# A graph network on one core: edge table stored before other loads, a shortened last edge batch, and moments of layer 3 taken one bank later

## The chip, the cores and the metric

The kernel runs on one core of a Trainium2 chip. The metric is device time in microseconds (us) of one execution; the time before is the median of three runs, 1525.76 us (1524.59 to 1526.87). The core has five instruction queues that run side by side and meet at semaphores: PE (matrix multiply), DVE (vector), ACT (scalar functions and copies), POOL (general purpose, here also the issuer of indirect gathers) and SP (here only an issuer of transfers). Transfers run on 16 DMA engines that all queues share.

## The reference: what is computed

The input is a graph of 3125 nodes with 128 features each and 103125 edges, sorted by destination: 50000 random edges, their reverses, and one loop per node. Four graph layers follow one another, each wrapped as `x = layernorm(x + layer(x))`:

```python
x = _layernorm(x + _L0_gnn_ref(x, src, dst, edge_weight, ...))   # weighted sum of x@W over edges, relu
x = _layernorm(x + _L1_gnn_ref(x, edge_index, ...))              # 4-head attention over edges, skip, norm
x = _layernorm(x + _L2_gnn_ref(x, Wq, Wk, Wv, Wo, edge_index))   # dot-product attention over edges
x = _layernorm(x + _L3_gnn_ref(x, edge_index, ...))              # two mean aggregations, sigmoid
```

All four layers use the same edges. Only layer 0 uses the edge weights.

## The kernel before, in words

The kernel does not gather per edge. It builds two dense 3200 x 3200 matrices in device memory (25 blocks of 128 nodes, the last one padded): `f_ctd`, the edge counts in bf16, and `wd`, the summed edge weights in f32. After that each layer is dense matrix products that stream blocks of these matrices back. If a check at the end fails (a flag), a general path is run instead; with these inputs it is not.

**The start (lines 543 to 652).** `src`, `dst` and the weights are loaded as 127 rows of 816 edges (line 583 and on). DVE and ACT form `tab`, which holds for each edge a key (destination times 25 plus source block), the source within its block, and the weight. `tab` is stored to device memory as `td` in two halves, one on SP's queue and one on ACT's (line 634). PE and DVE work out `row_i`, the row of `td` where each group of five destination nodes begins. Then POOL issues five indirect gathers (line 649), each of 128 runs of 256 consecutive edges, one run for each group. Three tiles hold the results, so the fourth and fifth gather wait for the first and second to be read. Before these gathers stand, in SP's order, the load of `x` (line 643) ahead of SP's half of `td`, and in ACT's order the loads of most of the weights (line 541, the helper `load`); POOL's order has `f_both` (line 729) ahead of the gathers.

**Keys (lines 654 to 697).** For each gather, `keys_of` transposes the edges of the 128 groups on PE and turns them into bf16 keys and three-part bf16 weights on ACT and DVE. The tables of the first two gathers are made before the batches start.

**The batches (lines 814 to 901).** The 640 groups are worked off in 40 batches of 16 (`NW`, `BW`, `NBT`). For a batch, `make` has DVE write two one-hot matrices (line 827: `ohd` for the source within its block, `ohc` for destination and source block) and three weighted copies `wod` of `ohd` (line 836); ACT writes a part of the third copy, 16 pieces a batch (line 845). PE then multiplies one-hots against one-hots: in each of four steps of four groups, 8 products for the counts (line 867) and 24 for the weights (line 875). ACT copies both out of PSUM (lines 880 and 886), and SP stores the weights of every batch (two transfers, line 888) and the counts of every two batches (line 891). The one-hots have two buffers, so DVE works at most one batch ahead of PE. Two jobs run beside the first batches: `xw_of` (x times the weight of layer 0; lines 750 to 756), called after the first and second batch in the program, and `products_of_weights` (lines 733 to 744), called after the third. In the order that the scheduler gave the engines, both begin before the first batch's products.

Meanwhile PE already does layer 0: `add0` loads a finished block row of `wd` in halves of 10 blocks (line 793, three buffers) and multiplies it into five PSUM banks (line 797). The last rows of `wd` are there only after the last batch. Groups beyond number 625 hold no node, since 3125 nodes are 625 groups of five: the last batch, groups 624 to 639, has one group with nodes.

**The end of layer 3 (lines 1563 to 1692).** 25 blocks of the output lie in eight PSUM banks (`GT`: five of four blocks, two of two, one of one). PE finishes the banks one after another. For each bank, `sigmoid` has DVE add the layer's own part (line 1581) and ACT take the sigmoid (line 1584); `total` has DVE add `x` (line 1589), `moments` has it take mean and variance (lines 1595 and 1596). `roots` is a chain of 13 small DVE instructions that finds inverse square roots of 8 or 4 variances by Newton steps; the last five blocks use ACT's square root instead, whose table has to be loaded first. `scaled` normalizes on ACT or DVE, and `store` writes 4 to 8 blocks to the output. The order of DVE and ACT here is written out by hand (`manual_schedule`); `mixed` interleaves two lists of instructions. Everywhere else a scheduler orders each engine, and `issue_after` places something behind a given instruction.

Of the kernel before, what the change touches and what calls it, by code (L numbers as in the profile page):

```python
# [15 lines left out]
P = 128  # L16
N = 3125
# [476 lines left out]
KW = WN * NB  # L494
NBT = NW // BW
Z0 = 20
V1 = 100
# [11 lines left out]
def fast_path(  # L509
# [29 lines left out]
    def load(name, ap, shape):  # L539
        t = cst.tile(shape, F32, name=name)  # L540
        nc.scalar.dma_start(t, ap)
        return t
# [32 lines left out]
    with ExitStack() as st:  # L575
# [66 lines left out]
        nc.vector.tensor_copy(ramp, ramp_i)  # L642
    nc.sync.dma_start(x[:, 0:NF, :], x_in[0 : NF * P, :].rearrange("(b p) d -> p b d", p=P))
    nc.gpsimd.memset(x[:, NF, :], 0.0)
    nc.sync.dma_start(x[0:NR, NF, :], x_in[NF * P : N, :])
    egs = []
    for g in range(NG):
        eg = ep.tile([P, EW // 16, 3, 16], F32, name="eg", bufs=3)
        nc.gpsimd.indirect_dma_start(
            out=eg.rearrange("p a t k -> p (a t k)"), out_offset=None, in_=td,  # L650
            in_offset=bass.IndirectOffsetOnAxis(ap=row_i[:, g : g + 1], axis=0),
        )
        egs.append(eg)

    def keys_of(g):
# [43 lines left out]

    l0_wt = load("f_l0_wt", l0_w, [P, P])  # L700
    l0_br = cst.tile([P, P], F32, name="l0_br")
# [10 lines left out]
    for s, a in enumerate((l1_as, l1_ad)):  # L712
        for h in range(H):
            nc.scalar.dma_start(att[h * C : (h + 1) * C, s * H + h : s * H + h + 1], a[h, :].rearrange("(c o) -> c o", o=1))
    wqt = load("f_wq", l2_wq, [P, P])
# [10 lines left out]
    wyv = cst.tile([P, 2 * P], F32, name="wyv")  # L726
    both = cst.tile([P, P], F32, name="f_both")
    def products_of_weights():
        nc.gpsimd.tensor_tensor(both, gb_row, sb_row, OP.add)
        tw = {}  # L730
        for name, w in (("l1", l1_wt), ("q", wqt), ("k", wkt), ("v", wvt)):
            t = zps.tile([P, P], F32, name="trw", tag="acc3")
            nc.tensor.transpose(t, w, ident)
            tw[name] = ep.tile([P, P], F32, name="tw_" + name)
            nc.scalar.copy(tw[name], t)
        t = zps.tile([P, P], F32, name="trw", tag="acc3")
        nc.tensor.matmul(t[:, 0 : 2 * H], tw["l1"], att, start=True, stop=True)
# [74 lines left out]
    wv_ = wd.rearrange("(w i) (c d) -> w (i c) d", i=WN, d=P)  # L812

    def make(b):
# [7 lines left out]
        def twos(k):  # L822
            k = k[:, b % 8, :, :, :].rearrange("p q w t -> p (q w) t")
            return k[:, :, None, :].to_broadcast([P, 2 * BW, P // 2, 2])

        for o, k in ((ohd, kd2), (ohc, kc2)):
            nc.vector.tensor_tensor(  # L827
                o.rearrange("p w (a t) -> p w a t", t=2), twos(k),
                ramp.rearrange("p (a t) -> p a t", t=2)[:, None, :, :].to_broadcast([P, 2 * BW, P // 2, 2]),
                OP.is_equal,  # L830
            )
        wod = []
        for s in range(3):
            f = of_.tile([P, 2 * BW, P], BF16, name="wod")
            n = 2 * BW if s < 2 else BW
            nc.vector.tensor_tensor(  # L836
                f[:, 0:n].rearrange("p w (a t) -> p w a t", t=2), ohd[:, 0:n].rearrange("p w (a t) -> p w a t", t=2),
                twos(w2[s])[:, 0:n], OP.mult,
            )
            wod.append(f)  # L840
# [14 lines left out]
    for b in range(NBT):  # L855
        ohd, ohc, wod, _ = cur
        cur = make(b + 1) if b + 1 < NBT else None
        if b % SB == 0:
            cs = sp.tile([P, NB, SB * BW * WN], BF16, name="cs")
        ws = sp.tile([P, BW, P], F32, name="ws")  # L860
        for k in range(0, BW, 4):
            cp = cps.tile([P, 4, P], F32, name="cp", tag="cw")
# [8 lines left out]
            for j in range(4):  # L871
                for q in range(2):
                    w = q * BW + k + j
                    for s in range(3):
                        nc.tensor.matmul(  # L875
                            wp[:, j, :], ohc[:, w, :], wod[s][:, w, :], start=(j == 0 and q == 0 and s == 0),
# [6 lines left out]
            )  # L883
            if cur:
                cur[3](k)
            nc.scalar.copy(ws[:, k : k + 4, :], wp)  # L886
        for a, e in ((0, 112), (112, KW)):
            nc.sync.dma_start(wv_[b * BW : (b + 1) * BW, a:e, :].rearrange("w k d -> k w d"), ws[a:e, :, :])
        if b % SB == SB - 1:
            i0 = (b - SB + 1) * BW * WN  # L890
            nc.sync.dma_start(ctd[:, :, i0 : i0 + SB * BW * WN].rearrange("c d i -> d c i"), cs)
        if b < 2:
            for blocks in GB[4 * b : 4 * b + 4]:
                xw_of(*blocks)
        if b == 2:
            products_of_weights()
            acc0 = [zps.tile([P, 4, P], F32, name=f"acc{k}", tag=f"acc{k}") for k in range(Z0 // 4)]
# [564 lines left out]
    with ExitStack() as st:  # L1462
# [135 lines left out]
        def some(name, n, d=F32):  # L1598
            return lp.tile([P, 8], d, name=name)[:, 0:n]

# [42 lines left out]
        by = {}  # L1643
        chain = []
        with tc.manual_schedule(engines={mybir.EngineType.DVE, mybir.EngineType.Activation}):
            for g in range(len(GT)):
                for b in range(NB - HB, NB):
                    add2(last[b], b, g)
                sigmoid(g)
                if g == 2:  # L1650
                    chain = roots(0, 8)
                elif g == 3:
                    scaled(0, 4)
                elif g == 4:
                    chain = roots(8, 8)
                    scaled(4, 4)
                    store(0, 8)
                elif g == 5:
                    scaled(8, 4)
                elif g == 6:  # L1660
                    chain = roots(16, 4)
                    scaled(12, 2)
                mixed(chain[:4])
                total(g)
                mixed(moments(g), chain[4:])
                chain = []
            n = 5
            va = some("var3", n)
            sd = some("sd3", n)
# [58 lines left out]
```

## Time and profile before

| what | us |
|---|---|
| median of three runs (lowest, highest) | 1525.76 (1524.59, 1526.87) |
| profiled execution, its own time | 1526.18 |
| its span in the trace | 1524.3 |
| PE busy, weight loads busy | 1394.6, 1221.3 |
| DVE busy, ACT busy, POOL busy | 984.4, 911.2, 127.3 |
| first gather issued | 22.93 |
| first one-hot begun on DVE | 31.82 |
| last count product begun on PE | 467.81 |
| last block rows of layer 0 in the first five banks | 488.26 to 499.65 |
| PE's last matrix product begun | 1503.28 |
| last store issued | 1517.57 |

The span is the time from the first to the last recorded instruction. Busy times are averages over stages with different limits: DVE is nearly always busy in the first third of the span and PE in the rest. A line of a timeline gives start, duration, engine, line of the kernel, operation, output and inputs, shape, how many instructions are merged into the line, and in brackets how long the engine had been idle and what ended that. A line of waits gives engine, tile and line, what was waited for, the total in us, how often and the longest. A line of windows gives a stretch, its length, the busy time and number of instructions of each engine, the granted clock of PE (1.00 is full speed), the mean busy share of the DMA engines and what they moved in GB/s. Releasers are inferred, so a wait for several things names the one that came last by the profile.

### The profile page before, as it was taken

The numbers are of one execution on the slowest core, as the hardware profiler recorded it, in microseconds if no ns is written. First come the engines' busy times: TensorE is split into PE (matmuls) and PEld (weight loads), VectorE is DVE, ScalarE is ACT, GpSimd is POOL, SyncE is SP. The second block draws the span as 40 slices with busy tenths as digits, with TensorE's granted clock in tenths as the row PEclk, the third lists the DMA queues.
The fourth block names the chain that finished last, engine by engine and source line by source line (L and its number), as shares of the span: only waits on it lengthen the run. The fifth ranks groups of instructions, "written<-read, shape, count | busy, mean of one in ns | idle before, by whom it ended". The sixth has DMA issues, their size and how long they took to land. (4 is left out here: it accounts for less than half of the span.)

```text
span 1524.3 us, 35229 instructions
## 1 busy us (share of the span) xinstructions
PE 1394.6 (91%) x14871; PEld 1221.3 (80%) x14871; DVE 984.4 (65%) x1602; ACT 911.2 (60%) x1864; POOL 127.3 (8%) x162
## 2 busy tenths in 40 slices
PE   4899999999997987899989989899999999999994
PEld 3898999898997876889979979677777774458994
DVE  4999999999991389869978878534464351012006
ACT  2988778888883479878778777454465331023003
POOL 2000000000000023113212311300000000000000
PEclk8999999999999999999999999999999999999997
DMA  6387887887878633444434433332222216503551
GB/s 194 83 214 212 217 219 206 236 219 196 227 211 252 204 103 98 143 122 122 130 120 117 131 91 108 119 114 68 68 61 79 79 65 249 203 32 136 200 186 45
DMA packets 210338, 223.92 MB, mean 147 GB/s; under 512 B 72861, under 2 KB 183976, under 8 KB 209914
## 3 DMA queue, kind: packets, MB, share of 16 engines
q1 hardware_dynamic: 206312, 217.26, 48.6%
q10 hardware_dynamic: 3457, 2.35, 0.6%
q8 instruction: 118, 1.93, 0.5%
q0 software_dynamic: 400, 1.97, 0.4%
q14 instruction: 51, 0.41, 0.1%
HBM read 157.19 MB, written 64.36 MB: 145 GB/s over the span
## 5 line engine op out<-in xcount | busy, mean ns | idle before, releaser
L1244 PE MATMUL acc<-vp,cm 128*128 128x198 bf16 x2500 | 344.4, 252 | 7.4 <-DVE cm L1229 4.6
L1228 ACT ACTIVATE fm<-adr,bas 128x896 bf16<-128x896 f32 (+1 forms) x320 | 286.2, 952 | 67.8 <-DVE cm L1229 63.0
L1239 PE MATMUL acc<-vp,ct 128*128 128x204 bf16 x1250 | 314.6, 255 | 8.5 <-DVE vp L1147 4.5
L1244 PEld LDWEIGHTS <-cm 128*128 128x128 bf16 x2500 | 235.6, 98 | 26.0 <-issue 8.7
L875 PE MATMUL wp<-wod,ohc 128*128 128x128 bf16 x3840 | 243.6, 219 | 7.0 <-ACT cs L880 6.6
L875 PEld LDWEIGHTS <-ohc 128*128 128x128 bf16 x3840 | 224.0, 98 | 8.3 <-issue 8.1
L836 DVE TENSOR_TENSOR wod<-ohd,w 128x4096 bf16<-128x4096 bf16 (+1 forms) x120 | 225.1, 1932 | 0.6 <-PE wp L875 0.6
L1229 DVE TENSOR_TENSOR cm<-fm,ct 128x896 bf16<-128x896 bf16 (+1 forms) x320 | 197.9, 649 | 35.7 <-PE acc L1244 14.6
L845 ACT ACTIVATE wod<-ohd,wu 128x128 bf16<-128x128 bf16 x640 | 197.0, 400 | 0.0
L1384 DVE TENSOR_TENSOR e<-e,ct 128x416 f32<-128x416 f32 (+1 forms) x175 | 108.3, 625 | 106.2 <-ACT e L1383 98.0
L1383 ACT ACTIVATE e<-s,f_nm 128x416 f32<-128x416 f32 (+1 forms) x175 | 109.6, 633 | 97.8 <-PE s L1380 88.7
L1388 PEld LDWEIGHTS acc<-self__8127,e 128*128 128x128 f32 x1250 | 148.3, 193 | 20.6 <-issue 18.8
L1388 PE MATMUL acc<-self__8127,e 128*128 128x129 f32 x1250 | 148.6, 276 | 0.5 <-DVE e L1384 0.5
L1380 PE MATMUL s<-yT,f_xT 128*128 128x416 f32 (+1 forms) x350 | 142.8, 543 | 4.6 <-ACT rt L1360 4.0
L797 PE MATMUL acc<-f_xw,cw 128*128 128x128 f32 x1000 | 119.2, 279 | 7.4 <-DMA cw<-wd 7.4
L1239 PEld LDWEIGHTS <-ct 128*128 128x128 bf16 x1250 | 122.4, 98 | 2.6 <-issue 1.5
L886 ACT COPY ws<-wp 128x512 f32<-128x512 f32 x160 | 93.7, 585 | 49.4 <-PE wp L875 47.9
L797 PEld LDWEIGHTS acc<-f_xw,cw 128*128 128x128 f32 x1000 | 115.8, 195 | 7.6 <-DMA cw<-wd 7.6
L867 PE MATMUL cp<-ohc,ohd 128*128 128x125 bf16 x1280 | 96.7, 218 | 22.2 <-ACT ws L886 18.2
L1380 PEld LDWEIGHTS s<-yT,f_xT 128*128 128x128 f32 x350 | 62.1, 191 | 55.5 <-issue 39.2
L827 DVE TENSOR_TENSOR ohd<-kd,ramp 128x4096 bf16<-128x4096 bf16 x40 | 91.6, 2290 | 21.7 <-PE cp L867 21.1
L1563 PEld LDWEIGHTS <-ct 128*128 128x128 bf16 x1875 | 104.9, 98 | 0.0
(298 smaller groups left out, 1497.1 us busy)
## 6 DMA issues: line engine op xcount, KB each, us to landing
ct<-f_ctd SPq DMA_DIRECT2D x48, 800.0 KB
wd<-ws SPq DMA_DIRECT2D x40, 896.0 KB
ct<-f_ctd SPq DMA_DIRECT2D x150, 224.0 KB
cw<-wd SPq DMA_DIRECT2D x50, 640.0 KB
f_ctd<-cs SPq DMA_DIRECT2D x20, 1000.0 KB
ct<-f_ctd SPq DMA_DIRECT2D x25, 416.0 KB
ct<-f_ctd SPq DMA_DIRECT2D x25, 365.2 KB
cw<-wd SPq DMA_DIRECT2D x25, 320.0 KB
```

What stands on the lines that cost most here:

```text
L797: nc.tensor.matmul(accs[j // 4][:, j % 4, :], cw[:, j - h, :], xw[:, i, :], start=False, stop=(i == NB - 1 and (j % 4 == 3 or j == n - 1)) ...
L836: nc.vector.tensor_tensor(f[:, 0:n].rearrange("p w (a t) -> p w a t", t=2), ohd[:, 0:n].rearrange("p w (a t) -> p w a t", t=2), twos(w2[s] ...
L845: nc.scalar.activation(wod[2][:, BW + w, :], ohd[:, BW + w, :], AF.Copy, scale=w3[:, 1, at : at + 1])
L875: nc.tensor.matmul(wp[:, j, :], ohc[:, w, :], wod[s][:, w, :], start=(j == 0 and q == 0 and s == 0), stop=(j == 3 and q == 1 and s == 2), ...
L1228: nc.scalar.activation(f[:, : n * P], at, AF.Relu, bias=bas[:, c, h : h + 1], scale=UP)
L1229: nc.vector.tensor_tensor(m[:, : n * P], f[:, : n * P], ct[:, : n * P], OP.min)
L1239: nc.tensor.matmul(out_(F1, PW), ct[:, k * P : (k + 1) * P], vp[:, c, hp : hp + 2, :, 2 * F1 : V1], start=(c == 0), stop=False, skip_group ...
L1244: nc.tensor.matmul(out_(0, 2 * F1)[:, j], ms[j][:, k * P : (k + 1) * P], vp[:, c, hp + j, :, 0 : 2 * F1], start=False, stop=(c == NB - 1 a ...
L1380: nc.tensor.matmul(s[:, :m], xT[:, c * P : (c + 1) * P], yT[:, i0 * P + a : i0 * P + a + m], start=True, stop=True)
L1383: nc.scalar.activation(e[:, a : a + m], s[:, :m], AF.Exp, bias=nm[:, q : q + 1], scale=scale)
L1384: nc.vector.tensor_tensor(e[:, a : a + m], e[:, a : a + m], ct[:, a : a + m], OP.mult)
L1388: nc.tensor.matmul(acc[k // 3][:, (k % 3) * (P + 1) : (k % 3 + 1) * (P + 1)], es[q, c][:, k * P : (k + 1) * P], vo[:, c, 0 : P + 1], start ...
```

## The change

There are three parts.

1. **Start.** The load of `x` and, behind it, nearly all weights move to SP's queue and behind the first two gathers; two small writes to `x` on POOL, placed behind the second gather, make the load of `x` wait for it. The weight and bias of layer 0 stay on ACT's queue. `xw_of` is placed behind the last product of batch 0 and of batch 1, and `products_of_weights` behind that of batch 2.
2. **Last batch.** It makes and multiplies 4 groups instead of 16 (`LW`): one step of PE instead of four, and narrower one-hots. The rows of `wd` that it no longer stores are filled with zeros by six transfers at the start, and the columns of `cs` that it no longer writes by one instruction on POOL. The store of the counts keeps its size.
3. **End of layer 3.** The moments of a bank come after the next bank's `sigmoid` part on DVE, ahead of its `total`. The chains of roots are two of eight blocks instead of two of eight and one of four, taken one bank later; the last nine blocks (five before) use ACT's square root. Which blocks are scaled on ACT and DVE, and where the stores stand, changes with that.

```diff
+LW = 4
+NL = (NBT - 1) * BW + LW
...
     def load(name, ap, shape):
         t = cst.tile(shape, F32, name=name)
-        nc.scalar.dma_start(t, ap)
+        with tc.issue_after(x_load.ins):
+            nc.sync.dma_start(t, ap)
         return t
...
-    nc.sync.dma_start(x[:, 0:NF, :], x_in[0 : NF * P, :].rearrange("(b p) d -> p b d", p=P))
-    nc.gpsimd.memset(x[:, NF, :], 0.0)
-    nc.sync.dma_start(x[0:NR, NF, :], x_in[NF * P : N, :])
     egs = []
     for g in range(NG):
         eg = ep.tile([P, EW // 16, 3, 16], F32, name="eg", bufs=3)
-        nc.gpsimd.indirect_dma_start(
+        got = nc.gpsimd.indirect_dma_start(
...
         egs.append(eg)
+        if g == 1:
+
+            with tc.issue_after(got.ins):
+                nc.gpsimd.memset(x[:, 0:1, 0:1], 0.0)
+                nc.gpsimd.memset(x[:, NF, :], 0.0)
+    x_load = nc.sync.dma_start(x[:, 0:NF, :], x_in[0 : NF * P, :].rearrange("(b p) d -> p b d", p=P))
+    nc.sync.dma_start(x[0:NR, NF, :], x_in[NF * P : N, :])
...
-    l0_wt = load("f_l0_wt", l0_w, [P, P])
+    l0_wt = cst.tile([P, P], F32, name="f_l0_wt")
+    nc.scalar.dma_start(l0_wt, l0_w)
...
-            nc.scalar.dma_start(att[h * C : (h + 1) * C, s * H + h : s * H + h + 1], a[h, :].rearrange("(c o) -> c o", o=1))
+            with tc.issue_after(x_load.ins):
+                nc.sync.dma_start(att[h * C : (h + 1) * C, s * H + h : s * H + h + 1], a[h, :].rearrange("(c o) -> c o", o=1))
...
+    none = ep.tile([P, 10 * NB], F32, name="none")
+    nc.vector.memset(none, 0.0)
+    for i in range(NL * WN, NP, 10):
+        with tc.issue_after(x_load.ins):
+            nc.sync.dma_start(wd[i : i + 10, :].rearrange("i k -> (i k)").rearrange("(p k) -> p k", p=P), none)
...
+        def some(s):
+            if b < NBT - 1:
+                return [slice(0, 2 * BW if s < 2 else BW)]
+            return [slice(0, LW)] + ([slice(BW, BW + LW)] if s < 2 else [])
...
+        nw = BW if b < NBT - 1 else LW
         if b % SB == 0:
             cs = sp.tile([P, NB, SB * BW * WN], BF16, name="cs")
+            if b + SB == NBT:
+                nc.gpsimd.memset(cs[:, :, ((SB - 1) * BW + LW) * WN :], 0.0)
         ws = sp.tile([P, BW, P], F32, name="ws")
-        for k in range(0, BW, 4):
+        for k in range(0, nw, 4):
...
-            if cur:
+            if cur and (b + 1 < NBT - 1 or k < LW):
                 cur[3](k)
...
-            nc.sync.dma_start(wv_[b * BW : (b + 1) * BW, a:e, :].rearrange("w k d -> k w d"), ws[a:e, :, :])
+            nc.sync.dma_start(wv_[b * BW : b * BW + nw, a:e, :].rearrange("w k d -> k w d"), ws[a:e, 0:nw, :])
...
         if b < 2:
-            for blocks in GB[4 * b : 4 * b + 4]:
-                xw_of(*blocks)
+            with tc.issue_after(made.ins):
+                for blocks in GB[4 * b : 4 * b + 4]:
+                    xw_of(*blocks)
         if b == 2:
-            products_of_weights()
+            with tc.issue_after(made.ins):
+                products_of_weights()
...
                 sigmoid(g)
-                if g == 2:
-                    chain = roots(0, 8)
-                elif g == 3:
+                if g in (3, 5):
+                    chain = roots(0 if g == 3 else 8, 8)
+                if g == 4:
                     scaled(0, 4)
-                elif g == 4:
-                    chain = roots(8, 8)
+                elif g == 5:
                     scaled(4, 4)
                     store(0, 8)
-                elif g == 5:
+                elif g == 6:
                     scaled(8, 4)
-                elif g == 6:
-                    chain = roots(16, 4)
-                    scaled(12, 2)
-                mixed(chain[:4])
+
+                mixed(left, chain)
+                chain = []
                 total(g)
-                mixed(moments(g), chain[4:])
-                chain = []
-            n = 5
+                left = moments(g)
+            n = 9
             va = some("var3", n)
             sd = some("sd3", n)
+            ms = some("ms3", n)
 
             nc.scalar.activation(some("root3", 1), deg[:, 0:1], AF.Sqrt)
-            scaled(14, 2)
+            scaled(12, 2)
+            mixed(left)
+            nc.vector.tensor_scalar(va, mv[:, 16:25, 1], EPS, None, OP.add)
+            nc.scalar.activation(sd, va, AF.Sqrt)
+            scaled(14, 2, True)
             store(8, 8)
-            nc.vector.tensor_scalar(va, mv[:, 20:25, 1], EPS, None, OP.add)
-            nc.scalar.activation(sd, va, AF.Sqrt)
-            scaled(16, 4, True)
+            nc.vector.reciprocal(sd, sd)
+            nc.vector.scalar_tensor_tensor(ms, mv[:, 16:25, 0], -1.0, sd, OP.mult, OP.mult)
+            for j in range(n):
+                by[16 + j] = sd[:, j : j + 1], ms[:, j : j + 1]
+            scaled(16, 4)
+            scaled(20, 5, True)
             store(16, 4)
-            nc.vector.reciprocal(sd, sd)
-            ms = some("ms3", n)
-            nc.vector.scalar_tensor_tensor(ms, mv[:, 20:25, 0], -1.0, sd, OP.mult, OP.mult)
-            for j in range(n):
-                by[20 + j] = sd[:, j : j + 1], ms[:, j : j + 1]
-            scaled(20, 3)
-            scaled(23, 2, True)
             store(20, 5)
```

More of the change, by code (lines that the diff above doesn't have):

```diff
@@ L824, in twos, with packed @@
             return k[:, :, None, :].to_broadcast([P, 2 * BW, P // 2, 2])
-        for o, k in ((ohd, kd2), (ohc, kc2)):
[L827 to L831, printed above, removed]
+        def some(s):
+            if b < NBT - 1:
+                return [slice(0, 2 * BW if s < 2 else BW)]
+            return [slice(0, LW)] + ([slice(BW, BW + LW)] if s < 2 else [])
+        def packed(o, ww):
+            return o[:, ww].rearrange("p w (a t) -> p w a t", t=2)
+        for o, k in ((ohd, kd2), (ohc, kc2)):
+            for ww in some(0):
+                nc.vector.tensor_tensor(
+                    packed(o, ww), twos(k)[:, ww],
+                    ramp.rearrange("p (a t) -> p a t", t=2)[:, None, :, :].to_broadcast(
+                        [P, ww.stop - ww.start, P // 2, 2]
+                    ),
+                    OP.is_equal,
+                )
         wod = []
@@ L834, in make @@
             f = of_.tile([P, 2 * BW, P], BF16, name="wod")
[L835 to L839, printed above, removed]
+            for ww in some(s):
+                nc.vector.tensor_tensor(packed(f, ww), packed(ohd, ww), twos(w2[s])[:, ww], OP.mult)
             wod.append(f)
@@ L874, in fast_path @@
                     for s in range(3):
-                        nc.tensor.matmul(
+                        made = nc.tensor.matmul(
                             wp[:, j, :], ohc[:, w, :], wod[s][:, w, :], start=(j == 0 and q == 0 and s == 0),
@@ L1598, in some @@
         def some(name, n, d=F32):
-            return lp.tile([P, 8], d, name=name)[:, 0:n]
+            return lp.tile([P, 9], d, name=name)[:, 0:n]
         def roots(b0, n):
@@ L1644, in fast_path @@
         chain = []
+        left = []
         with tc.manual_schedule(engines={mybir.EngineType.DVE, mybir.EngineType.Activation}):
```

## The prediction

> **What bounds the kernel now.** The page's chain of work that ended last is no help here: it holds two pieces, both at 1517 us, and breaks off. I read the stages instead, first by windows, then by timeline, at the three places that the change touches.
>
> The start. In the windows of one microsecond the DMA engines are full from 11 to 20 us; they carry the table `td` (1.25 MB), but also `x` (1.57 MB), which stands ahead of one half of `td` on SP's queue, and weights. The row at 10 us is 0.85 full at only 78 GB/s: there the bias rows are copied to all partitions in pieces of 512 bytes.
>
> ```profile
> 10.00:11.00 1.00, 0.00 (x0) 0.00 (x0) 1.00 (x7) 0.87 (x1) 0.50 (x1) 1.00 0.85 78
> ...
> 13.00:14.00 1.00, 0.83 (x4) 0.84 (x5) 0.00 (x0) 0.11 (x1) 0.00 (x0) 1.00 1.02 313
> ...
> 19.00:20.00 1.00, 0.00 (x0) 0.00 (x0) 0.00 (x0) 0.00 (x0) 0.00 (x0) 1.00 0.96 365
> 20.00:21.00 1.00, 0.47 (x2) 0.47 (x3) 0.00 (x0) 0.00 (x0) 0.00 (x0) 1.00 0.50 186
> ```
>
> The timeline shows who waits. `row_i` is ready at 17.06, yet the first gather goes out at 22.93: it waits for `td` (the profile names another transfer, but in the program the gather waits only for `td` and `row_i`). DVE waits for the second gather until 29.95, and the one-hots begin at 31.82.
>
> ```profile
> 16.89 0.17 DVE L641 TENSOR_SCALAR row_i<-cnt 128x5 int32<-128x5 f32 x1
> ...
> 22.93 1.20 POOL L649 DMA_INDIRECT eg<-td,row_i  x1 [11.20 <-DMA f_att<-in_L_gnn_att_dst_dram]
> ...
> 29.95 0.35 DVE L662 TENSOR_SCALAR kic<-eg,thr 128x256 f32<-128x256 f32 x1 [2.23 <-DMA eg<-td,row_i]
> ...
> 31.82 2.28 DVE L827 TENSOR_TENSOR ohd<-kd,ramp 128x4096 bf16<-128x4096 bf16 x1
> ```
>
> From there to 150 us DVE (third column) is the bound, with ACT behind it; later DVE loses some 7% to waits for PE:
>
> ```profile
> 50.00:100.00 50.00, 45.78 (x696) 44.35 (x694) 49.47 (x32) 44.35 (x126) 0.00 (x0) 1.00 0.65 164
> 100.00:150.00 50.00, 45.10 (x696) 44.05 (x694) 49.83 (x31) 44.90 (x129) 0.00 (x0) 1.00 0.79 211
> 150.00:200.00 50.00, 47.28 (x719) 46.77 (x718) 45.52 (x26) 39.80 (x110) 0.00 (x0) 1.00 0.80 213
> ```
>
> So a start that is earlier by some microseconds moves everything behind it, if ACT keeps up.
>
> The last batch. Its four steps on PE end near 470; SP can store its weights only at 474.5, since it stands until then before a buffer for `cw`; behind that store (1000 KB) and the counts (1000 KB) comes the load that PE waits for, 7.42 us without work. After it PE runs slower: 11.39 us for 80 instructions that took 9.20 before.
>
> ```profile
> 467.81 0.60 PE L867 MATMUL cp<-ohc,ohd 128*128 128x125 bf16 x8
> ...
> 471.64 9.20 PE L797 MATMUL acc<-f_xw,cw 128*128 128x128 f32 x80
> 474.50 3.24 SPq L888 DMA_DIRECT2D wd<-ws  x2
> 477.79 1.37 SPq L891 DMA_DIRECT2D f_ctd<-cs  x1
> 479.26 22.64 SPq L793 DMA_DIRECT2D cw<-wd  x9
> ...
> 488.26 11.39 PE L797 MATMUL acc<-f_xw,cw 128*128 128x128 f32 x80 [7.42 <-DMA cw<-wd]
> ```
>
> The end. PE begins its last products at 1503.28, DVE still has 13 us to go and waits 0.7 us for ACT's sigmoid in most banks:
>
> ```profile
> 1487.89 0.63 ACT L1584 ACTIVATE t<-t 128x512 f32<-128x512 f32 x1 [87.31 <-DVE t L1581]
> 1488.55 0.69 DVE L1589 TENSOR_TENSOR f_xw<-t,f_x 128x512 f32<-128x512 f32 x1 [0.69 <-ACT t L1584]
> ...
> 1517.57 0.87 SPq L1634 DMA_DIRECT2D out_dram<-f_x  x1
> ```
>
> **Part 1, the start: 4.0 us earlier.** With `x` and the weights gone, `td` is alone. Its first half is issued at 12.32; 1.25 MB at the 380 GB/s of the rows from 17 to 20 us are 3.3 us; bytes begin to flow about 1 us behind an issue, and the gather came 2.3 us behind the last full row: 18.9. The edges themselves also land sooner, which can move `td` and `row_i` up by about 1.7 (DVE waited 4.61 for `src`, between weight loads): 17.2 for `td`, and 15.4 for `row_i`, below which it can't go. I take 17: 6 us. Ends 4.0 and 7.5. The second gather should keep its 5.5 us to landing: `x` now starts beside it, the weights are gone.
>
> What that newly leans on: `x` waits on SP for the second gather's issue, and behind `x` stand 24 weight transfers and six zero fills of 128 KB, ahead of batch 0's store. Their bytes fall into 35 to 50 us, where the DMA share was 0.00 to 0.02. ACT's order now has the copies of the third and fourth gather ahead of the rest of the second key table and of the first counts copy. At 300 GB/s `x` and three gathers of 0.4 MB are 9 us from about 19, so 28 to 29, when DVE needs them at 28: at most 1 us, inside the ends.
>
> The price: `xw_of` and the weight products were partly done before 46 us, while ACT had gaps. Now all 14 copies at 0.47 from start to start and seven at 0.3, 8.7 us, lie in batches 1 to 3; before, 4.2 us of them did, with DVE never stalled. Four or five of the copies also wait for their products on PE (four took 0.71 at 41.57). So about 7.5 us more. A batch takes DVE 9.9 us (43.42 to 53.36) and ACT 8.6 (16 pieces in 4.8, eight copies at 0.47), leaving 1.3 a batch or 4 over three batches; the second one-hot buffer gives 2 to 4 more (PE's last step of batch 1 ends at 61.0; DVE needs its buffers at 63.3 and 65.5). 7.5 - 4 - 2 is 1.5; I take 2. Ends 0 and 6. No earlier row shows the new order, hence the wide ends.
>
> **Part 2, the last batch: 7.0 us earlier.** Three steps of PE go, 462.09 to 467.81, 5.7 us; DVE's one-hots (10.2 us a batch) and 12 pieces on ACT shrink too, but DVE was done at 461.7, so PE's count is the one that matters. PE then starts the block row of 471.6 at 466, frees the buffer, and SP gets on at about 469. But the DMA engines are full to 473 (0.92 to 1.12 in the windows) and still have 0.66 MB of `cw` to bring, to about 475. Then 0.25 + 1.0 + 0.64 MB at the 294 GB/s of 476 to 488 are 6.6 us, and about 1 to land: 482.5 in place of 488.26, 5.8 us. Without any backlog it would be 480; if only the smaller store counted (0.75 MB, 2.6) and the idle stretch of 473 to 476 (0.38 busy, 1.9), 4.5. PE's wait shrinks from 7.4 to about 4.5 us. In the trace the granted clock averaged 0.68 over 485 to 488, so it fell at about 486, 5.2 us into the wait; a shorter one may keep it, and then 80 instructions take 9.2 in place of 11.4. I count half: 1.2. Ends of the part: 4.5 and 9.
>
> The Trainium skill, "TensorE: Matmul & The Clock Gate", Part 1, speaks against that half: the array drops to half rate after an idle window of about 3.4 us, and windows run free. A 4.5 us wait would then often still end cold, which makes the part 5.8 and not 7.0. At the end of the kernel the trace agrees with the shorter time (PE stops at 1504.3, 0.66 over 1506 to 1508), in the wait at 481 it took longer.
>
> The zero column fill on POOL costs nothing (POOL idles from 32 to 470, 437.67 us); `none` is written while DVE waits 4.61 us for `src`. If those covers went, it would be under 2 us.
>
> **Part 3, the end: 1.4 us earlier.** Walking DVE with the rows' times (sums 1.0 for four blocks, total 0.65, moments 1.07, a chain of 13 with moments 2.9): banks 1 to 3 start when PE frees them (1490.1, 1493.5, 1496.9); bank 3 with its chain ends at 1501.4, bank 4 at 1504.15, bank 5 with a chain at 1507.9, bank 6 at 1509.4. Bank 7's sigmoid now stands behind four `scaled` on ACT: total at 1511.0 (before 1513.8). Then the table load (1.28), two `scaled`, the root at 1513.1, reciprocal and product to 1513.7, four `scaled` on ACT to 1515.4 beside five on DVE. The last compute ends at 1515.4 in place of 1517.5, but two stores follow (0.87 and 1.1 us of SP), so the last issue ends 0.9 earlier; of the 17 blocks that were stored behind 1515.7 at 290 GB/s, eight now go 2.5 us sooner. I take 1.4; ends 0 and 2.5.
>
> **Sum.** 6.0 - 2.0 + 7.0 + 1.4 = 12.4. The profiled execution took 1526.18 (span 1524.3 and 1.88 around it), so 1513.8; the median stands 0.42 lower: 1513.4. The order of the engines between 500 and 1480 us is as before, so the gain should pass through.
>
> **Rivals.**
> - *All works out* (0.20): ACT's backlog is absorbed, PE stays warm: 7 + 8.5 + 2 = 17.5, 1508.3. For it: no stall of DVE from 43 to 75 us. Against: twice the copies there.
> - *The start is given back* (0.15): ACT's backlog stalls DVE for all 6 us: 7 + 1.4, 1517.4. For it: ACT is at 89% there already.
> - *SP's list comes too late* (0.05, slower): the 30 transfers behind `x` hold batch 0's store. With two `ws` buffers, ACT stalls once that store is not over by about 59, so the list must end by 53, 34 us after `x`: about 1.05 us each. On ACT's queue the weights took 0.44 to 0.5 each, the first four `att` transfers 6.08, 1.52 each. If all took 1.52, the list would take 52 us, 18 too long: 12.4 gained, 18 lost, 1531. It decides at about 1.4 each.
> - *Next to nothing* (0.05): the start is given back and the wait for `cw` stays, so only scraps remain: within 0.2%.
>
> **The numbers.** My forecast has 0.55. The range 1506.5 to 1519.5 takes in the first two rivals and most of the ends, about 8 in 10. Faster by more than 0.2% (3 us, about what a measurement of this kernel can tell from no change): 0.90; within: 0.05; slower: 0.05.
>
> **What would show it.** The first gather at 16 to 18.5; the first one-hot at about 26; DVE's wait for PE or ACT between 45 and 80 us (new, under 3 us in sum, if I am right); PE's wait for `cw` at the end of layer 0 shorter than 5.5 us, with its clock telling whether it stayed warm; one-hot products ending near 460; the last store issued near 1516.5 less the shift. I'm wrong if the first gather still waits beyond 20, if `ws` is late for SP's list, or if the batches after 150 us run slower than 11 us each.

## The result, and the profile after

The changed kernel takes 1524.79 us (median of 14 runs, 1523.01 to 1528.32) and the kernel before 1526.11 us (14 runs beside them). The ratio is 0.9993 with a 95% interval of 0.9986 to 1.0001: no difference that can be told. The forecast was 1513.4, in a range from 1506.5 to 1519.5.

The profiled execution after has a span of 1521.5 us (1524.3 before), 2.8 us shorter. It took 1523.26 us, 1.5 less than its median, so about half of these 2.8 us is the scatter of single executions. Where they come from:

| place | before | after | later (+) or earlier (-) |
|---|---|---|---|
| first gather issued | 22.93 | 19.51 | -3.42 |
| DVE's first one-hot, batch 0 | 31.82 | 28.03 | -3.79 |
| DVE's first one-hot, batch 7 | 104.65 | 109.94 | +5.29 |
| DVE's first one-hot, batch 39 | 451.72 | 456.27 | +4.55 |
| last rows of layer 0 end in the first five banks | 499.65 | 498.19 | -1.46 |
| PE's last bank begun | 1503.28 | 1501.01 | -2.27 |
| last compute instruction ends | 1517.55 | 1512.79 | -4.76 |
| end of the span | 1524.3 | 1521.5 | -2.8 |

So the start gains 3.8 us, loses 9.1 by batch 7, and the last batch gives some 6 back. The lines below answer to those shown of before. First the windows of the kernel after (stretch, length, PE, PEld, DVE, ACT, POOL, clock, DMA share, GB/s):

```profile
11.00:12.00 1.00, 0.67 (x2) 0.50 (x2) 0.80 (x4) 0.04 (x1) 0.00 (x0) 1.00 0.73 157
...
13.00:14.00 1.00, 1.00 (x7) 1.00 (x6) 0.00 (x0) 0.00 (x0) 0.00 (x0) 1.00 1.35 274
...
15.00:16.00 1.00, 0.68 (x3) 0.69 (x4) 0.86 (x5) 0.00 (x0) 0.00 (x0) 1.00 0.02 10
...
17.00:18.00 1.00, 1.00 (x7) 1.00 (x6) 0.00 (x0) 0.00 (x0) 0.00 (x0) 1.00 0.71 294
...
50.00:100.00 50.00, 46.93 (x630) 44.20 (x630) 42.19 (x29) 42.51 (x120) 0.00 (x0) 1.00 0.58 151
```

`td` is alone on the DMA engines now, yet its 1.25 MB take from 11 to 18 us, with a hole at 15. The two halves, 64 packets of 9.8 KB each, moved one behind the other. The rows by queue show it (queue, kind, packets, MB, share of the 16 engines' time; q1 carries what SP issues, q10 what ACT issues). First the kernel after from 11 to 14.5 us and from 14.5 to 18.2:

```profile
q1 hardware_dynamic: 64, 0.63, 86.4%
...
q10 hardware_dynamic: 82, 0.63, 86.9%
```

Before, both queues moved at once, here from 18 to 20 us, at 379 GB/s together. 75 of these 151 packets are larger than 8 KB, as those of `td` are (9.8 KB), and they make up 0.73 of the 0.76 MB:

```profile
q1 hardware_dynamic: 57, 0.43, 59.1%
q10 hardware_dynamic: 94, 0.32, 40.7%
```

SP's half was issued at 10.41 instead of 12.32. ACT's half stands behind other work of ACT, and its issue ended at 13.84 in both kernels; first before, then after:

```profile
13.34 0.50 ACTq L634 DMA_DIRECT2D td<-tab  x1
```

```profile
12.37 1.47 ACTq L637 DMA_DIRECT2D td<-tab  x1
```

DVE, busy for 49.47 of the 50 us from 50 to 100 before, has only 42.19, and ACT, with 42.51, isn't full either. The waits of DVE from 45 to 100 us (what waited, for what, total, times, longest) name the reason, first before, then after:

```profile
DVE ohd L827 <- ACT wod L845: 0.5, 1, 0.5
```

```profile
DVE ohd L851 <- PE cp L893: 7.8, 4, 3.0
```

The timeline of the kernel after at the places that were shown of before:

```profile
19.51 1.20 POOL L649 DMA_INDIRECT eg<-td,row_i  x1 [17.06 <-DMA td<-tab]
...
22.18 0.82 SPq L659 DMA_DIRECT2D f_x<-in_x_dram  x1
...
28.03 2.29 DVE L851 TENSOR_TENSOR ohd<-kd,ramp 128x4096 bf16<-128x4096 bf16 x1
...
30.62 0.40 ACT L677 COPY wei<-eg 128x256 f32<-128x256 f32 x1 [2.25 <-DMA eg<-td,row_i]
...
63.97 2.29 DVE L851 TENSOR_TENSOR ohd<-kd,ramp 128x4096 bf16<-128x4096 bf16 x1 [1.89 <-PE cp L893]
...
79.28 0.27 ACT L751 COPY tw_q<-trw 128x128 f32<-128x128 f32 x1 [0.42 <-PE trw L749]
...
471.68 4.73 PE L813 MATMUL acc<-f_xw,cw 128*128 128x128 f32 x40 [1.17 <-DMA cw<-wd]
479.00 4.73 PE L813 MATMUL acc<-f_xw,cw 128*128 128x128 f32 x40 [2.59 <-DMA cw<-wd]
487.36 10.83 PE L813 MATMUL acc<-f_xw,cw 128*128 128x128 f32 x80 [3.62 <-DMA cw<-wd]
...
1513.34 0.40 SPq L1661 DMA_DIRECT2D out_dram<-f_x  x1
```

ACT's copy of the third gather stands ahead of the second key table and waits 2.25 us, since `x` now moves beside that gather. Each weight product is one step of PE and one copy of ACT in turn (ACT waits 0.42 to 0.58 us ahead of most of these copies of 0.17 to 0.27 us). DVE waits for one-hot buffers that PE frees late. At the end of layer 0 PE waits three times (7.4 us in sum, as before), but starts its last rows 0.9 us sooner than before although DVE reached batch 39 4.55 us later.

### The profile page after: what moved, and what is told of

It reads as the page before. It is cut to its first block, busy times and chain, and to the rows that moved or that the text cites. A ratio compares the mean times of both kernels' runs of the same rounds, so it can differ in the third digit from the quotient of the medians.

```text
span 1521.5 us, 35026 instructions
## 1 busy us (share of the span) xinstructions
PE 1387.3 (91%) x14762; PEld 1214.9 (80%) x14775; DVE 975.9 (64%) x1595; ACT 903.8 (59%) x1845; POOL 129.3 (8%) x164
## 5 line engine op out<-in xcount | busy, mean ns | idle before, releaser
L862 DVE TENSOR_TENSOR wod<-ohd,w 128x4096 bf16<-128x4096 bf16 (+2 forms) x122 | 221.3, 1867 | 0.6 <-PE wp L901 0.6
L851 DVE TENSOR_TENSOR ohd<-kd,ramp 128x4096 bf16<-128x4096 bf16 (+1 forms) x41 | 90.0, 2196 | 28.2 <-PE cp L893 27.9
```

The costliest lines, as they stand in the source:

```text
L862: nc.vector.tensor_tensor(packed(f, ww), packed(ohd, ww), twos(w2[s])[:, ww], OP.mult)
```

## The experiments

Theory A: part 1 gains 3.8 us and pays more than that, because the copies of `xw_of` and of the weight products were moved out of ACT's idle time into the first batches; parts 2 and 3 gain. Rival B: part 1 comes out even and part 2 gains nothing, its wait being bound by transfers. Ratios are to the kernel before on the same chip, and "us to before" is the ratio's share of the median of before. A column named "batch 39" is the start of DVE's first one-hot of that batch in the trace.

**Each part alone.** The first three runs take the change apart, the fourth is parts 2 and 3 together. Where part 1 is out, the zero fills are issued behind the first store of batch 0.

```diff
# e1: part 1 of the diff above alone
# e2: part 2 alone, e4: parts 2 and 3, both with the fills placed so:
-        with tc.issue_after(x_load.ins):
+    if b == 0:
+        with tc.issue_after(put.ins):   # put: the second store of ws
             nc.sync.dma_start(wd[i : i + 10, :]..., none)
# e3: part 3 alone
```

> The kernel before with part 1 alone (edges first, `x` behind the second gather, weights behind `x`, `xw_of` and the weight products behind the last one-hot products of their batches). Theory A (the start gains 3.8 us and the moved copies stall DVE for more than that): DVE's first one-hot 3.8 us sooner, its one-hot of batch 39 about 4.5 us later than before, and the kernel +4.5 us, ratio 1.003. Rival B (part 1 comes out even, and it is part 2 that gains nothing): 0 us, ratio 1.000. The prediction on record (6.0 gained, 2.0 paid): -4 us, ratio 0.9974.

> The kernel before with part 2 alone (the last batch holds four groups; the zero fills of the table are issued behind the first store of batch 0). Theory A: the step is worth 5.5 us of earlier landing of `cw` and 0.5 us of faster products behind it, so -6 us, ratio 0.9961. Rival B (the wait for `cw` is bound by the transfers, since its sum over three waits is 7.4 us as before): 0 to -1 us. The prediction on record: -7 us, ratio 0.9954.

> The kernel before with part 3 alone (moments a bank behind in layer 3's end). Theory A (the last compute ends 2.5 us sooner against PE's last bank, but the stores behind it end only 0.5 us sooner): -0.5 us, ratio 0.9997, not to be told from 1. The prediction on record: -1.4 us, ratio 0.9991. Rival: the new order of the end costs more than it brings, 0 to +1 us.

> Parts 2 and 3 without part 1 (zero fills behind the first store of batch 0). Theory A: -6.5 us, ratio 0.9957, some 5 us faster than the whole change. Rival B (part 2 gains nothing): -0.5 to -1.5 us, like the whole change, ratio 0.9993.

| run | ratio (95%) | us to before | batch 39 |
|---|---|---|---|
| part 1 | 1.0053 (1.0039 to 1.0067) | +8.1 | 456.55 |
| part 2 | 0.9982 (0.9972 to 0.9992) | -2.7 | 453.68 |
| part 3 | 0.9983 (0.9974 to 0.9992) | -2.6 | 451.42 |
| parts 2 and 3 | 0.9965 (0.9952 to 0.9977) | -5.3 | 453.20 |

Part 1 alone makes the kernel slower, so both rival B and the prediction fall; it costs more than theory A said (+4.8 us at batch 39 in its trace as expected, +2.4 more at the end, see below). Part 2 gains half of what was expected, part 3 five times. The trace of parts 2 and 3 tells one reason why part 2 falls short: up to batch 8 it runs with part 3 alone (114.41 and 114.28), and by batch 10 it is 2.6 us behind (137.03 and 134.38). There the scheduler gave PE another order: 40 products of layer 0 in one piece. The PE timeline of parts 2 and 3, and behind it that of part 3 alone:

```profile
120.21 4.68 PE L803 MATMUL acc<-f_xw,cw 128*128 128x128 f32 x40
```

```profile
106.81 2.45 PE L797 MATMUL acc<-f_xw,cw 128*128 128x128 f32 x20
119.11 2.45 PE L797 MATMUL acc<-f_xw,cw 128*128 128x128 f32 x20
```

DVE waits 2.6 us for PE between 105 and 140 us in the first and not at all in the second. Part 2 alone has the long piece too, and 24.2 us from batch 8 to batch 10 where before has 20.1. The changed kernel has a third order, without this loss. That is one reason why the three parts, measured alone, add to +2.8 us and not to the -1.1 of the whole.

**Where part 1 loses.** Four runs move one thing each in the changed kernel.

```diff
# e5: both freed; e6: xw_of alone; e7: the weight products alone
-            with tc.issue_after(made.ins):
-                for blocks in GB[4 * b : 4 * b + 4]:
-                    xw_of(*blocks)
+            for blocks in GB[4 * b : 4 * b + 4]:
+                xw_of(*blocks)
-            with tc.issue_after(made.ins):
-                products_of_weights()
+            products_of_weights()
# e8: x behind the third gather
-        if g == 1:
+        if g == 2:
```

> The kernel after without the ordering of `xw_of` and the weight products behind the batches' products; `x` and the weights still come late. Theory A (the placement behind batches 0 to 2 stalls DVE for 7.4 us, while ACT is without work for 7.7 us between 25 and 45 us): DVE's one-hot of batch 39 5 to 7 us earlier than after (456.27), the kernel 1524.8 - 6 = 1519, ratio 0.995 to before. Rival C (it is the load order that costs: copies in the gaps then wait for `x` and weights that land at 30 to 46 us and stall the key tables): DVE no earlier than after, ratio 0.999 or above.

> The kernel after with `xw_of` alone freed, the weight products still behind batch 2. Theory A: the losses at batches 3 and 4 (2.9 and 1.4 us) go, the 3.0 us at batch 5 stay: DVE at batch 39 4.3 us earlier than after, about 1520.5, ratio 0.9965. Rival C: no earlier than after, 0.999 or above.

> The kernel after with the weight products alone freed, `xw_of` still behind batches 0 and 1. Theory A: the 3.0 us at batch 5 go, the 4.3 us at batches 3 and 4 stay or grow to 5: DVE at batch 39 2 to 3 us earlier than after, about 1522.3, ratio 0.9975. Rival C: 0.999 or above.

> The kernel after with `x` behind the third gather in place of the second. Theory A: the third gather lands 2 us sooner (ACT's copy of it ended DVE's wait at batch 0's second one-hot, 2.0 us); the later `x` costs nothing as `xw_of` stands behind batch 0 in any case: DVE 1 to 2 us earlier at batch 39, ratio 0.998 to 0.999. Rival C (late `x` is what stalls ACT and PE): 1 to 2 us later than after, ratio 1.000.

| run | ratio (95%) | us to before | batch 0 | batch 1 | batch 3 | batch 7 | DVE waits, 45 to 100 us |
|---|---|---|---|---|---|---|---|
| before | 1 | 0 | 31.82 | 43.42 | 63.30 | 104.65 | 0.5 |
| after | 0.9993 (0.9986 to 1.0001) | -1.1 | 28.03 | 41.16 | 63.97 | 109.94 | 7.8 |
| both freed | 0.9973 (0.9964 to 0.9983) | -4.1 | 28.25 | 41.11 | 61.34 | 106.34 | 4.3 |
| `xw_of` freed | 0.9983 (0.9974 to 0.9992) | -2.6 | 28.33 | 41.28 | 61.17 | 106.04 | 3.9 |
| products freed | 0.9998 (0.9989 to 1.0007) | -0.3 | 27.73 | 40.54 | 63.77 | 108.57 | 7.1 |
| `x` behind the third gather | 0.9981 (0.9971 to 0.9990) | -2.9 | 27.85 | 39.73 | 63.58 | 109.56 | 8.9 |

Freeing `xw_of` brings 3.9 us by batch 7, near the 4.3 expected. But 2.4 of them are lost again between batches 7 and 10 (32.72 us for 30.28), where DVE waits 1.9 us for ACT and 0.8 for PE, so that batch 39 comes only 1.4 us earlier. Freeing the products alone brings 1.4 us by batch 7 and nothing at batch 39, 457.05 (expected 2 to 3). With both free DVE still waits 4.3 us, and even then stands 1.7 us behind the kernel before at batch 7: half of theory A holds, and so does half of rival C, as I read it because the copies cannot start before `x` is there. (The profiled execution with both freed took 1528.11 us beside a median of 1523.11, so its later rows are not read.) With `x` behind the third gather the 1.5 us between batches 0 and 1 are won, and most of them lost again at batch 3, where DVE waits longer. So a sooner start only meets the same backlog sooner. The ratio of this run lies where it was expected (0.998 to 0.999), but its interval overlaps with that of the kernel after, and its trace has batch 39 only 0.6 us earlier (expected 1 to 2).

**Can `x` come early and the start too?** And what does the order of parts 2 and 3 cost?

```diff
# e9: parts 2 and 3; zero fills placed behind the first one-hots
+                hot = nc.vector.tensor_tensor(...)            # make, ohd and ohc
+        if b == 0:
+            with tc.issue_after(hot.ins):
+                ...zero fills...
# e10: the kernel after, both freed, x directly behind SP's half of td
+        with tc.issue_after(first_half.ins):
+            x_load = nc.sync.dma_start(x[:, 0:NF, :], ...)
# e11: as e10, and in load():
-        with tc.issue_after(x_load.ins):
-            nc.sync.dma_start(t, ap)
+        with tc.issue_after(stored.ins):
+            nc.scalar.dma_start(t, ap)
```

> Parts 2 and 3 without part 1 as before, but the six zero fills of the table stand behind the first one-hot and not behind batch 0's store. Theory A: parts 2 and 3 alone lost 2.9 us in batches 8 to 10 because the fills behind batch 0's store changed the order that the planner gives PE there (20 products of layer 0 in one place in place of 10 and 10); with the fills earlier that order is as before, so DVE stands at batch 39 as before (451.5 within 0.5) and the kernel gains 5.6 + 2.0 = 7.6 us, ratio 0.995. Rival E (the loss belongs to the shorter last batch or is chance): as in parts 2 and 3 before, DVE at batch 39 near 453.5, ratio 0.9965.

> The kernel after with `x` directly behind its queue's half of `td` (no wait for the second gather) and `xw_of` and the weight products free; weights, zero fills and parts 2 and 3 as after. Theory A (it is the late `x`, that moves 14 copies out of ACT's gaps, that gives the start back): `x` lands near 21 us, first gather near 19.5, first one-hot near 28.5, DVE's waits for PE between 45 and 100 us under 1 us, DVE at batch 39 at 448 to 449.5 (3 us before the kernel before), and the kernel 3 + 5.6 + 2 - 1.7 (the longer end that the runs with part 1 show) = 9 us faster than before, ratio 0.994. Rival D (ACT's work of 44 of 50 us is what stalls DVE once the start is earlier, wherever the copies stand): DVE waits 3 to 5 us there again, batch 39 at 452 to 454, ratio 0.997.

> The same as the run before it, but 16 weight transfers are issued by ACT behind its half of `td` and not by SP. SP then has 515 instructions in place of 530 (the kernel before has 514). Theory A for the end: the time from the last issue of a store to the end of the span, 7.5 to 7.9 us in all runs with part 1 and 5.7 to 6.4 in all without, goes with SP's longer program (a last fetch of instructions stands alone at the end), so it is 5.7 to 6.4 here, and the kernel 1.5 us faster than the run before it, ratio 0.993. Rival F (the end's length has another cause): 7.5 to 7.9. The 16 issues take ACT 7 us between 13 and 24, where it has no other work: no loss, or up to 1 us.

In the second and third of these the last block of `x` is set to zero behind its load, so the features of the last 53 nodes are left out and the result is not that of the reference.

| run | ratio (95%) | us to before | first gather | batch 0 | batch 7 | batch 39 |
|---|---|---|---|---|---|---|
| fills behind the one-hots | 0.9966 (0.9953 to 0.9979) | -5.2 | 23.44 | 34.23 | 106.44 | 453.52 |
| `x` behind `td` | 0.9956 (0.9942 to 0.9969) | -6.7 | 23.52 | 31.77 | 105.14 | 452.19 |
| weights on ACT | 0.9975 (0.9967 to 0.9984) | -3.8 | 22.04 | 34.29 | 107.60 | 455.55 |

The first run has PE's order of before, and the 2.6 us between batches 8 and 10 are gone (116.39 to 136.48, 20.1 us as before). But the fills did not wait for the one-hots: `issue_after` orders SP's list, and with no data to wait for SP issued them at once, beside the first two gathers, so that batch 0 began 2.1 us later than with part 3 alone. Its timeline:

```profile
19.83 4.57 SPq L851 DMA_DIRECT2D wd<-none  x6
23.44 1.20 POOL L651 DMA_INDIRECT eg<-td,row_i  x1 [12.13 <-DMA td<-tab]
...
34.23 2.29 DVE L841 TENSOR_TENSOR ohd<-kd,ramp 128x4096 bf16<-128x4096 bf16 x1
```

So the run ends where its rival E had put it (batch 39 near 453.5, ratio 0.9965), for another reason.

The second run missed its start (first gather expected near 19.5). Its timeline:

```profile
10.10 0.54 SPq L637 DMA_DIRECT2D td<-tab  x1
11.08 0.83 SPq L641 DMA_DIRECT2D f_x<-in_x_dram  x1
...
23.52 1.20 POOL L655 DMA_INDIRECT eg<-td,row_i  x1 [21.06 <-DMA td<-tab]
```

On SP's own queue `x` kept its turn: SP's half of `td` moved from 11 to 14 us, and `x` from there. But the other half, issued by ACT at 12.06, moved only from 18.4 to 22, behind and beside the rest of `x`. These are the rows of ACT's queue from 14 to 18.4 us and from 18.4 to 22:

```profile
q10 hardware_dynamic: 2, 0.00, 0.1%
...
q10 hardware_dynamic: 79, 0.63, 42.5%
```

The first gather, which needs both halves, is back at 23.5, and DVE's waits are back at 0.6 us. In these runs, either `x` moves ahead of ACT's half of `td` and the gather is late, or `x` comes behind the gathers and the copies are late. No run put `x` directly behind both halves, and none had both early, so rival D (a stall even with early copies, once the start is earlier) was not decided by this one.

The third run was expected 1.5 us faster than the second and is slower. The 16 issues kept ACT until 31.87 (expected 24), and its copies for the first key table stand behind them, so batch 0 began at 34.29 although the first gather went out at 22.04.

**The copies left out, and the best version.**

```diff
# e12: the kernel after; in products_of_weights and xw_of, six places like
-            nc.scalar.copy(tw[name], t)
+            nc.gpsimd.memset(tw[name], 0.0)
# e13: parts 2 and 3; the zeros are written behind the last gather
+    with tc.issue_after(got.ins):
+        nc.gpsimd.memset(none, 0.0)
# (the six fills follow, with no order of their own)
```

> The kernel after without the copies of `xw_of` and of the weight products: GpSimd fills their results with zeros at the start instead, so that layer 0's output, layer 1's attention and layer 2's products are computed from zeros; the products on TensorE stand where they stood. Theory A (those 21 copies on ACT, and PE's waiting for them, are the whole 7.4 us that DVE loses in batches 3 to 5): DVE's waits for PE between 45 and 100 us fall from 7.8 to under 1 us, its one-hot of batch 39 comes 6 to 7.5 us earlier than after (449 to 450), the kernel 6 to 7 us faster than after, ratio 0.995. Rival G (the load order and the third gather cost it, not the copies): DVE waits 4 us or more there still, batch 39 at 453 or later.

> Parts 2 and 3 without part 1, the zero fills waiting for the issue of the last gather (GpSimd writes their zeros behind it). Theory A: no fill beside the first two gathers (which cost the run with early fills 2.1 us at the first one-hot) and PE's order in batches 8 to 10 as before: first one-hot near 32, batch 39 at 451.5, the kernel 5.6 + 2.0 = 7.6 us faster than before, 1519, ratio 0.995. Rival E (the loss moves elsewhere again): 0.9965 as in the two runs before it with parts 2 and 3.

| run | ratio (95%) | us to before | batch 0 | batch 7 | batch 39 |
|---|---|---|---|---|---|
| copies left out | 0.9941 (0.9924 to 0.9957) | -9.0 | 28.04 | 103.26 | 449.76 |
| fills behind the gathers | 0.9957 (0.9945 to 0.9969) | -6.6 | 32.16 | 104.38 | 451.45 |

Without the copies batch 39 comes 6.5 us earlier than after, as theory A expected. DVE's waits fall from 7.8 to 2.6 us, not to under 1; the remaining 2.6 us I put down to the products themselves, which still lie between those of the batches, but that was not tried. Rival G falls: of the 9.1 us lost between batches 0 and 7, the copies account for 6.7. The DVE waits of this run, 45 to 100 us:

```profile
DVE ohd L851 <- PE cp L893: 2.6, 2, 1.6
```

The last run does as expected up to batch 39 (batch 0, batch 39 and the fills at 32.89), and has the lowest ratio of those that compute the reference: 1520.76 us, against 1526.76 for the kernel before beside it. It leaves the start as it was and takes parts 2 and 3. From batch 39 to the end of layer 0's last rows it gains 4.1 us, not the 5.6 expected. Its lead over the earlier run with parts 2 and 3 is not shown: it is 1.75 us ahead at batch 39, but its span is 1.0 us longer (1520.4 for 1519.4), and the two intervals overlap.

**The end.** From the end of the last store's issue to the end of the span it took 5.7 to 6.5 us in the seven kernels in which SP issues 506 to 520 transfers (before, parts 2, 3, 2 and 3, and e9, e11, e13), and 7.5 to 8.1 us in the eight in which it issues 530 to 536 (after, part 1, e5 to e8, e10, e12). The transfers of the last microseconds differ. First the kernel after, from 1515.5 us on in 40 slices, then parts 2 and 3 from 1513.5 (GB/s in each slice):

```profile
GB/s 47 129 22 69 22 22 22 22 3 0 0 0 0 0 0 0 50 0 0 0 0 0 0 0 0 0 0 0 0 50 0 0 0 0 0 0 0 0 0 0
q14 instruction: 5, 0.04, 2.1%
```

```profile
GB/s 265 277 284 299 296 299 211 50 44 28 69 72 69 22 22 22 22 3 0 0 0 0 0 0 0 0 50 0 0 0 0 0 0 0 0 0 0 0 0 0
q14 instruction: 4, 0.03, 1.8%
```

When the output has landed, two single fetches of instructions follow in the kernel after, some 2.1 us apart, and only one without part 1. Moving 16 issues from SP to ACT took the time from 8.1 (e10) to 6.5 us (e11), which speaks for the length of SP's program as the cause, with theory A for the end; that the second fetch is one of SP's is not shown. From PE's last bank to the end it is 21.02 us before, 18.87 to 19.11 in the four runs with part 3 and without part 1, 23.38 with part 1 alone and 20.49 in the whole change. So part 3 gains some 2.0 us by itself, and the whole change keeps 0.5 of them.

## Why the prediction was wrong

**The reading of what bounds the start was right:** a lead at the first one-hot passes on wherever nothing else comes between (in e8 4.0 us at batch 0 and 3.7 at batch 1), and what was lost in the first batches was still there at batch 39 (5.3 us late at batch 7, 4.6 at batch 39).

**Part 1, the first gather (6.0 forecast, 3.4 measured).** The mis-sized term is the time of `td`: 1.25 MB at 380 GB/s were to take 3.3 us, and took 7 (about 180 GB/s), although nothing else moved. The rate had been read in rows in which both halves moved at once; with a rate of that kind the sum needs both halves early, and it looked at SP's issue alone. ACT's issue ended at 13.84 as before, the halves moved one behind the other, and each took 3 to 3.5 us for 0.63 MB. Why one half alone is no faster stays open, and no run issued ACT's half sooner. `row_i` came at 16.11 (15.4 forecast) and did not bind.

**Part 1, the price (2.0 forecast, ends 0 and 6).** This is the step that failed: "7.5 - 4 - 2 is 1.5; I take 2". The copies were there, but the two cushions did not hold. The 1.3 us of ACT's time in each batch and the second one-hot buffer count only if copies can be fitted in without holding PE, and behind the batches' products they alternate with PE: ACT itself was idle for 7.5 of the 50 us from 50 to 100 while DVE waited. From batch 0 to batch 7 the lead went from 3.8 to -5.3: 1.5 us by the third gather and the rest as waits of DVE for PE. These 9.1 us lie outside both ends. Leaving the copies out (e12) gave 6.7 back, and moving `x` behind the third gather (e8) gave the 1.5 back, until batch 3. The rival "the start is given back" named the mechanism; it stopped at zero, while the part alone costs 8.1 us.

**Part 2 (7.0 forecast).** PE comes to the `left` products 5.84 us sooner after batch 39 (18.70 before, 12.86 after), the 5.7 us of three steps. From batch 39 to the end of the last rows it is 41.92 us for 47.93, so 6.0; in the eleven other profiles with part 2 the gain is 1.8 to 7.1, with 5.6 in the middle. The size holds, a little too high, with a scatter that in four of them falls to the lower end of 4.5 or below it. The share for the clock was 1.2 and measured 0.56 after a wait of 3.62 us. The last 80 products took 9.20 us behind waits of 1.68 and 2.15 (e7, e12), and 10.6 to 12.0 in every kernel with a wait of 3.3 us or more. The Trainium skill, "TensorE: Matmul & The Clock Gate", Part 1, says that an idle window of about 3.4 us halves the rate. These rows of 80 products agree, so counting half of the cold clock's price as saved was too much. The rows of 40 products fit it less well: in eight profiles they took 6.2 to 6.4 us in place of 4.73, behind waits from 1.19 us (e2, where the granted clock was 0.50 from 469 to 472) to 3.48, while in e11 they stayed at 4.73 behind 3.19. The length of the last wait alone does not decide it:

```profile
469.11 6.27 PE L803 MATMUL acc<-f_xw,cw 128*128 128x128 f32 x40 [1.19 <-DMA cw<-wd]
```

PE's waits for `cw` did not shrink in sum (7.4 us, forecast below 5.5), as the transfers end the last one.

**Part 3 (1.4 forecast).** 2.0 us by itself, 0.5 left of it in the whole change, whose end is the longer one of part 1. A gain was in the sum that another part's end takes away; no step looked at what follows the last store.

**The sum.** +4.5 at batch 39, -6.0 in the last batch, -0.8 between layer 0 and PE's last bank, -0.5 at the end: -2.8, the difference of the two profiled executions (1.3 between the medians). The -0.8 is scatter: that stretch took 1002.6 to 1006.2 us in the fifteen profiles, with no order to it that I found; it stays open. "SP's list comes too late" did not happen: the list of 32 transfers took 24.0 us, 0.75 each, ended at 46.2, and batch 0's store went out at 53.40. (At the feared 1.52 each, 32 are 49 us and not 52.)

## What to carry to other kernels

Before moving work out of an early idle stretch, ask for which engine that stretch was free room; the room is gone once the work is late, however much of it the later stages seem to have on average, and a chain of product and copy that alternates between two engines costs both. A rate is read together with what was moving: two halves on two queues are a fast transfer only while both move, so ask when each of them can be issued. And an order written for a scheduler is not a wait: where a transfer must keep clear of another, it needs data that are written late (e13), and a place in one queue says nothing about transfers on another (e10).

## What the runs showed of the hardware

- A store of 1.25 MB in two halves on two queues, issued 2 us apart (10.41 and 12.37), moved one half behind the other at about 180 GB/s with nothing beside it, with one microsecond at 10 GB/s in between. In the kernel before, both halves moved at once, at 379 GB/s from 18 to 20 us.
- A transfer on one queue can hold up one on another that is issued 1 us later: in e10 `x` was issued on SP's queue at 11.08 and moved from 14 us on, behind SP's half of `td`; ACT's half, issued at 12.06, moved only from 18.4 to 22, and the gather that needs both went out at 23.52, where it was 19.51 in the kernel after.
- The end of the span lies 5.7 to 6.5 us behind the end of the last store's issue in kernels in which SP issues 506 to 520 transfers, and 7.5 to 8.1 us where it issues 530 to 536.
- The granted clock fell to 0.50 at the end of a wait of 1.19 us in one profile (e2) and stayed at 1.00 behind one of 3.19 us in another (e11).
